# Layer 0 of a graph network on one core: the early part of the sums by source is put ahead of the second biases' rows

## The chip, the cores and the metric

The kernel runs on one core of one Trainium2 chip. The metric is the device time of one execution in microseconds, given as the median of several runs. Before the change it is 4813.85 us, the median of 3 runs (4810.83 to 4815.78).

## The reference

The program computes a network of four layers on 3125 nodes with 256 features and 100,000 edges. Each layer adds a graph convolution and an attention-like mix to the node features `x`, and then a feed-forward part. The change lies in the feed-forward part of layer 0, which is a mixture of 16 experts of which each node takes 2:

```python
gate_logits = x @ gate_w + gate_b
topk_vals, topk_idx = jax.lax.top_k(gate_logits, K)          # K = 2 of E = 16
topk_w = jax.nn.softmax(topk_vals, axis=-1)
h = jax.nn.relu(jnp.einsum('bsh,ehf->bsef', x, w1) + b1)
expert_out = jnp.einsum('bsef,efh->bseh', h, w2) + b2
sel = jnp.take_along_axis(expert_out, topk_idx[:, :, :, None], axis=2)
moe = jnp.sum(topk_w[..., None] * sel, axis=2)
y = x + moe
return (y - mu) / jnp.sqrt(var + EPS) * gamma + beta
```

Here `x` is the layer-normed input (`xn` in the kernel). One more piece is made in this stage although it belongs to layer 2: the graph convolution there needs the mean norm of all messages, `sum(|edge_weight| * norm(h[src])) / edges`. The kernel computes it as a sum over nodes, for which it needs, for every node, the sum of |edge_weight| over the edges that leave it. These are the "sums by source". They depend on the inputs alone, so they can be made at any time.

## The kernel before, in words

The nodes lie as 25 blocks of 125 (`NB`, `P`); `self.x` and `self.xn` are 125 x 25 x 256 in SBUF. The kernel is written with a tile framework: the program gives the operations, and a scheduler lays them into one queue for each engine at compile time. It takes the earlier operation in the program first where several are ready by its own clock, and may take a later one where the earlier ones still wait. Semaphores are added afterwards. On the chip each engine works off its queue in the order laid down.

`l0_ffn` (L1050) goes through these steps:

- The gates' best two (`top2`, L1062) and the place of each choice in a list sorted by expert (L1064 to L1114). The result is `slot` (L1114), 125 x 2 x 25 row numbers. The list is cut into 26 tiles of 384 rows (`NT`, `TS`), each tile belonging to one expert.
- The scatters (L1117): 50 indirect DMAs on GpSimd, one for each block and choice, write the rows of `xn` into `bx` in DRAM (`b0x_d` in the profile).
- `add_rows(beta)` (L1122, helper at L978): seven additions of `beta` to `x` on VectorE (L982).
- `times_rows` (L1124, helper at L285), called here "the second biases' rows": for seven pieces of four blocks it transposes the gates `g` (L291), copies them out of PSUM as `gt` (L293, recorded as L163 on VectorE or L165 on ScalarE), multiplies by the 16 x 256 matrix `b2` (L297), and adds the result to `xn` in place (L298). The addition to a block has to wait until both scatters of that block have read it.
- The early part of `weights_by_source` (L1128 to L1134, generator at L509). Its setup (L521 to L533) cuts weights and source numbers into bf16 keys. Then come groups of four columns of edges, 196 in all. Each group is five operations on VectorE (`lo` L537, `oh` L539, `ow` three times L543, each with three buffers) and four matmuls (L545) into one PSUM bank `ps`. The generator stops after each group; here it is run on until its share passes `EARLY` = 0.25. The block stands in `tc.issue_after(placed.ins)`, which puts its VectorE operations behind L1114 on VectorE and says nothing about other engines.
- The expert loop (L1142), 26 tiles. SP's queue is in program order here (`manual_schedule`, L1137): for each tile the loads of `w1`, `b1`, `w2` and of `xb` from `bx` (L1145 to L1151). TensorE transposes `xb` (L1156, 6 for each tile), VectorE copies to `xbt` (L1158), TensorE makes the hidden layer (L261), ScalarE its relu (L1163), TensorE the second product (L1168), and `evac` copies it out (L163 or L165) for a store to `by` (L1171). After each tile the loop advances the sums by source by their share (L1172).
- The gathers of `by` (L1180) with the weighting (L1183), and the closing norm.

PSUM is used in two pools of four banks: `self.bank()` (L150), from which `times_rows` and the sums take theirs, and the loop's own `pl` (L1136).

```python
placed = nc.vector.tensor_scalar(slot, sf, float(NT * TS - 1), None, op0=OP.min)
```

Of the kernel before, what the change touches and what calls it, by code (L numbers as in the profile page):

```python
# [109 lines left out]
class Net:  # L110
    NE, TS = 16, 384
# [938 lines left out]
    def l0_ffn(self, fast=False):  # L1050

        nc, tc, a = self.nc, self.tc, self.a
        NE, TS, ST, NT, bx = self.NE, self.TS, self.TS // 128, self.NT, self.bx
        by = self.dram.tile([NT * TS, D], F32, name="b0y_d")
        with ExitStack() as s:
            sb = s.enter_context(self.pool("f0_sb"))
            wk = s.enter_context(self.pool("f0_wk", 2))
            b2 = sb.tile([NE, D], F32, name="b2")
            nc.scalar.dma_start(b2, a["L0_ffn_b2"])
            gamma = self.load_b(sb, "L0_ffn_gamma")  # L1060
            beta = self.load_b(sb, "L0_ffn_beta")
            g, w, i8 = self.top2(sb, None, NE, P, NB, self.greatest)  # L1062
# [52 lines left out]
            for b in range(NB):  # L1115
                for j in range(2):
# [2 lines left out]
                        in_=self.xn[:, b, :], in_offset=None, bounds_check=NT * TS - 1, oob_is_err=False)  # L1119
                    tc.declare_no_dep(st.ins, group="slots", reason="each choice has a slot of its own")  # L1120
                    tc.add_to_no_dep_group("slots", st.ins)
            self.add_rows(beta)  # L1122
            y = self.xn
            self.times_rows(sb, g, b2, NE, y, self.xn)  # L1124
            with ExitStack() as s2:
                sums = None
                if fast:
                    sums = self.weights_by_source(s2.enter_context(self.pool("w_sb")),  # L1128
                                                  s2.enter_context(self.pool("w_wk", 3)), self.bank())

                    with tc.issue_after(placed.ins):
                        for part in sums:
                            if part > EARLY:
                                break  # L1134
                wk2 = s2.enter_context(self.pool("f0_t", 3))
                pl = s2.enter_context(self.pool("f0_ps", 4, space=PSUM))  # L1136
                s2.enter_context(tc.manual_schedule(engines={mybir.EngineType.SP}))  # L1137

                def bank():
                    return pl.tile([128, 512], F32, name="pl")  # L1140

                for i in range(NT):  # L1142
                    e = nc.sync.value_load(own[0:1, i:i + 1], min_val=0, max_val=NE - 1)
                    w1 = wk2.tile([128, HB, 512], F32, name="w1")
                    nc.sync.dma_start(w1, a["L0_ffn_w1"][ds(e, 1)].rearrange("o (c p) f -> p (o c) f", p=128))  # L1145
                    b1 = wk2.tile([128, 4], F32, name="b1")
                    nc.sync.dma_start(b1, a["L0_ffn_b1"][:, ds(e, 1), :].rearrange("p o f -> p (o f)"))
                    w2 = wk2.tile([128, 4, D], F32, name="w2")
                    nc.sync.dma_start(w2, a["L0_ffn_w2"][ds(e, 1)].rearrange("o (c p) f -> p (o c) f", p=128))
                    xb = wk2.tile([128, ST, D], F32, name="xb")  # L1150
                    nc.sync.dma_start(xb, bx[i * TS:(i + 1) * TS].rearrange("(t p) d -> p t d", p=128))  # L1151
                    xt = wk2.tile([128, HB, TS], F32, name="xbt", bufs=2)
                    for h in range(HB):
                        ps = bank()
                        for t in range(ST):
                            nc.tensor.transpose(ps[:, t * 128:(t + 1) * 128], xb[:, t, h * 128:(h + 1) * 128],  # L1156
                                                self.ident)
                        nc.vector.tensor_copy(xt[:, h, :], ps[:, :TS])  # L1158
                    hid = wk2.tile([128, 4, TS], F32, name="hid", bufs=2)
                    for f in range(4):  # L1160
                        ps = bank()
                        self.mm_feat(ps[:, :TS], w1[:, :, f * 128:(f + 1) * 128], xt, 0, TS)
                        nc.scalar.activation(hid[:, f, :], ps[:, :TS], AF.Relu, bias=b1[:, f:f + 1])  # L1163
                    yb = wk2.tile([128, ST, D], F32, name="yb", bufs=2)
                    for t in range(ST):
                        ps = bank()
                        for f in range(4):
                            nc.tensor.matmul(ps[:, :D], hid[:, f, t * 128:(t + 1) * 128], w2[:, f, :],  # L1168
                                             start=(f == 0), stop=(f == 3))
                        self.evac(yb[:, t, :], ps[:, :D])  # L1170
                    nc.scalar.dma_start(by[i * TS:(i + 1) * TS].rearrange("(t p) d -> p t d", p=128), yb)  # L1171
                    for part in sums or ():  # L1172
                        if i + 1 < NT and part > EARLY + (1 - EARLY) * (i + 1) / NT:
                            break
# [1250 lines left out]
```

## Time and profile before

| what | value |
|---|---|
| median of 3 runs | 4813.85 us |
| the profiled execution's own time | 4666.18 us |
| its span, first to last instruction | 4664.4 us |
| mean granted TensorE clock | 0.869 |
| busy share of PE / DVE / ACT / POOL | 80% / 54% / 28% / 22% |
| scatters (L1117) | 50, first at 808.71 us, last at 885.62 us |
| first transposes of the expert loop (L1156) | 892.9 us |
| first matmul of the expert loop (L261) | 926.8 us |
| last matmul of the expert loop (L1168) | 1274.0 us |

The profile shows one execution. Times are microseconds from the first instruction. PE is TensorE, PEld its weight loads, DVE VectorE, ACT ScalarE, POOL GpSimd and SP SyncE; a "q" after the name stands for the instructions of an engine's sequencer, such as the issue of a DMA. A row of the timeline gives start, busy time, engine, line, operation, output and inputs, how many were merged, and in brackets how long the engine was idle ahead of it and what released it. The profiled execution is 147.7 us shorter than the median of the runs that are only timed, so times of the profile are compared with times of the profile.

### The profile page before, as it was taken

The numbers are of one execution on the slowest core, as the hardware profiler recorded it, in microseconds if no ns is written. First come the engines' busy times: TensorE is split into PE (matmuls) and PEld (weight loads), VectorE is DVE, ScalarE is ACT, GpSimd is POOL, SyncE is SP. The second block draws the span as 40 slices with busy tenths as digits, with TensorE's granted clock in tenths as the row PEclk, the third lists the DMA queues.
The fourth block names the chain that finished last, engine by engine and source line by source line (L and its number), as shares of the span: only waits on it lengthen the run. The fifth ranks groups of instructions, "written<-read, shape, count | busy, mean of one in ns | idle before, by whom it ended". The sixth has DMA issues, their size and how long they took to land. (4 is left out here: it accounts for less than half of the span.)

```text
span 4664.4 us, 50401 instructions
## 1 busy us (share of the span) xinstructions
PE 3722.3 (80%) x16695; PEld 2505.9 (54%) x16695; DVE 2505.6 (54%) x8604; ACT 1302.8 (28%) x2336; POOL 1020.2 (22%) x1041
## 2 busy tenths in 40 slices
PE   1887796499938799999656566766799999999698
PEld 0676695277724556555545455655464444444466
DVE  5877317544475526994322323444265666777544
ACT  1367100022213223323100000000155655555521
POOL 2000000400055000000577777775000000000011
PEclk9786896599959799999877777887899999999699
DMA  6244630244332000000333333334102222221232
GB/s 176 75 113 118 138 82 22 81 135 140 107 85 40 4 29 9 13 14 7 106 105 106 104 104 104 104 104 139 58 7 59 59 63 56 63 52 49 74 107 68
DMA packets 256035, 358.86 MB, mean 77 GB/s; under 512 B 62719, under 2 KB 199350, under 8 KB 255765
## 3 DMA queue, kind: packets, MB, share of 16 engines
q1 hardware_dynamic: 135900, 176.07, 13.1%
q0 software_dynamic: 62832, 126.93, 10.3%
q10 hardware_dynamic: 57033, 52.54, 4.2%
q8 instruction: 136, 2.23, 0.2%
q14 instruction: 134, 1.10, 0.1%
HBM read 268.73 MB, written 94.97 MB: 78 GB/s over the span
## 5 line engine op out<-in xcount | busy, mean ns | idle before, releaser
L1601 POOL DMA_INDIRECT hg<-hx_d,idx x782 | 743.3, 950 | 282.8 <-issue 214.2
L1617 PE MATMUL acc<-hg,to 128*125 128x256 f32 x2042 | 584.5, 449 | 197.9 <-DVE to L1612 192.8
L1617 PEld LDWEIGHTS acc<-hg,to 128*125 128x125 f32 x2042 | 455.4, 227 | 309.3 <-DVE to L1612 216.3
L1971 PE MATMUL acc<-z,xr 125*65 125x500 f32 (+1 forms) x1400 | 577.4, 556 | 14.3 <-DVE z L1968 13.0
L1965 ACT ACTIVATE t<-xn,us 125x1000 f32<-125x1000 f32 (+1 forms) x400 | 409.4, 1037 | 239.0 <-DVE z L1968 228.1
L1968 DVE SCALAR_TENSOR_TENSOR z<-t,us,cs 125x1000 f32<-125x1000 f32 (+1 forms) x400 | 409.3, 1028 | 115.5 <-PE acc L1971 92.6
L1971 PEld LDWEIGHTS acc<-z,xr 125*65 125x65 f32 x1400 | 188.9, 145 | 314.8 <-issue 265.5
L1605 DVE TENSOR_TENSOR kw<-hg,awt 128x8 f32<-128x8 f32 x98 | 16.4, 168 | 581.2 <-DMA hg<-hx_d,idx 513.2
L261 PE MATMUL ps<-xt,w 128*128 128x500 f32 (+1 forms) x672 | 269.0, 547 | 1.8 <-DMA w<-in_L_ffn_W_dram 1.8
L1612 DVE TENSOR_SCALAR to<-iota_w,rel_b,kw 128x125 f32<-128x125 f32 (+1 forms) x782 | 245.2, 383 | 35.6 <-PE acc L1617 28.7
L1536 DVE SCALAR_TENSOR_TENSOR junk<-iota_w,rel_b,lock 128x125 f32<-128x125 f32 (+1 forms) x782 | 248.1, 386 | 0.0
L2255 POOL DMA_INDIRECT bx_d<-row,slot x25 | 31.2, 1248 | 891.3 <-ACT t L1965 422.9
L589 PE MATMUL ps<-y,cb 125*125 125x256 bf16 x1875 | 214.7, 279 | 0.0
L589 PEld LDWEIGHTS <-cb 125*125 125x125 bf16 x1875 | 213.5, 141 | 0.1
L797 ACT ACTIVATE k<-k 125x128 f32<-125x128 f32 x50 | 15.9, 318 | 687.0 <-DVE k L796 686.9
L190 ACT ACTIVATE rstd_t<-rstd_t 125x4 f32<-125x4 f32 (+2 forms) x86 | 17.2, 203 | 645.8 <-DVE rstd_t L189 630.2
L255 PE MATMUL ps<-wo,h 128*125 128x256 f32 x800 | 187.7, 386 | 3.6 <-ACT h L1439 2.6
L243 PE MATMUL ps<-ident,xn 125*128 125x125 f32 x300 | 58.8, 347 | 159.8 <-DVE xn L209 159.7
L1445 DVE SCALAR_TENSOR_TENSOR x<-ps,lg,x 125x256 f32<-125x256 f32 x200 | 92.7, 480 | 173.6 <-PE ps L255 173.6
L261 PEld LDWEIGHTS ps<-xt,w 128*128 128x128 f32 x672 | 122.7, 193 | 114.7 <-issue 102.4
L261 PE MATMUL ps<-h,w 128*128 128x500 f32 (+1 forms) x448 | 179.5, 541 | 2.3 <-ACT h L1434 1.6
L255 PEld LDWEIGHTS ps<-wo,h 128*125 128x125 f32 x800 | 142.9, 187 | 65.9 <-ACT h L1439 43.7
(566 smaller groups left out, 6326.7 us busy)
## 6 DMA issues: line engine op xcount, KB each, us to landing
cs<-ctt_d SPq DMA_DIRECT2D x150, 218.8 KB
w<-in_L_ffn_w_dram SPq DMA_DIRECT2D x52, 512.0 KB
cnt_d<-cd SPq DMA_DIRECT2D x25, 683.6 KB
cb<-cnt_d SPq DMA_DIRECT2D x25, 683.6 KB
ctt_d<-ct ACTq DMA_DIRECT2D x6, 2734.4 KB
hg<-hx_d,idx POOLq DMA_INDIRECT x782, 2.8
b0x_d<-zero SPq DMA_DIRECT2D x1, 9984.0 KB
xb<-b0x_d SPq DMA_DIRECT2D x26, 384.0 KB
```

Source lines behind the costliest of these rows:

```text
L243: self.nc.tensor.transpose(ps[:, j * P:(j + 1) * P], src[:, i // P + j, h * 128:(h + 1) * 128], self.ident[:P, :P])
L255: self.nc.tensor.matmul(ps, xt[:, h, b * P:(b + 1) * P], w[:, h, :], start=(h == 0), stop=(h == k - 1))
L261: self.nc.tensor.matmul(ps, w[:, h, :], xt[:, h, i:i + n], start=(h == 0), stop=(h == k - 1))
L589: nc.tensor.matmul(ps[:P, :D], cf[k][:, h * P:(h + 1) * P], y3[:, b0 + k, j, :], start=(k == 0 and j == 0), stop=(k == m - 1 and j == 2))
L1445: nc.vector.scalar_tensor_tensor(self.x[:, b, :], ps[:P, :D], g[:, b, e:e + 1], self.x[:, b, :], op0=OP.mult, op1=OP.add)
L1536: nc.vector.scalar_tensor_tensor(junk[:, :m * P], self.iota_w[:, :m * P], rel[:, c:c + 1], lock[:, b:b + m].rearrange("p b n -> p (b n)"), ...
L1601: nc.gpsimd.indirect_dma_start(out=hg[:, j, :], out_offset=None, in_=hx, in_offset=bass.IndirectOffsetOnAxis(ap=idx[:, c0 + j:c0 + j + 1], ...
L1612: nc.vector.tensor_scalar(to, self.iota_w[:, :nb * P], rel[:, c:c + 1], kw[:, j:j + 1], op0=OP.is_equal, op1=OP.mult)
L1617: nc.tensor.matmul(acc[k], to[:, (k - b) * P:(k - b + 1) * P], hg[:, j, :D], start=(c == first[k]), stop=(c == last[k]))
L1965: nc.scalar.activation(t[:, :n], rows[:, k4, :n], AF.Relu, bias=us[:, 2, b, k4:k4 + 1], scale=us[:, 0, b, k4:k4 + 1])
L1968: nc.vector.scalar_tensor_tensor(z[:, :n], t[:, :n], us[:, 1, b, k4:k4 + 1], c, op0=OP.add, op1=OP.mult)
L1971: nc.tensor.matmul(acc[h, k][:, :w], xr[:, b, k4, :], z[:, k * PW:k * PW + w], start=(b == 0), stop=(b == NB - 1))
```

## The change

The calls of `add_rows` and `times_rows` move from the place ahead of the early part of the sums to the place behind it, still ahead of the expert loop and its pools. Nothing is added or taken away.

```diff
-            self.add_rows(beta)
             y = self.xn
-            self.times_rows(sb, g, b2, NE, y, self.xn)
             with ExitStack() as s2:
                 sums = None
                 if fast:
...
                         for part in sums:
                             if part > EARLY:
                                 break
+                self.add_rows(beta)
+                self.times_rows(sb, g, b2, NE, y, self.xn)
                 wk2 = s2.enter_context(self.pool("f0_t", 3))
                 pl = s2.enter_context(self.pool("f0_ps", 4, space=PSUM))
                 s2.enter_context(tc.manual_schedule(engines={mybir.EngineType.SP}))
```

In program order the operations are then: the scatters, the sums' setup and 49 of their groups, the seven additions of `beta`, the biases' rows, the expert loop. Two things follow from the order of calls itself: the sums' PSUM bank is taken from `self.bank()` ahead of those of `times_rows`, and the two pools of the sums (`w_sb`, `w_wk`) are open while `times_rows` runs.

## The prediction

> **What bounds the kernel now.** I read the page first for the share of each engine, then the busy time by stretches around the edit, then the queues of VectorE (DVE), TensorE (PE) and SyncE (SP) in order of time. On the page PE is busy 80% of a span of 4664.4 us, but the edit touches one stage only, so that stage decides. By stretches (busy us, granted clock, DMA share, GB/s):
>
> ```profile
> core 0: us, PE busy (x) PEld busy (x) DVE busy (x) ACT busy (x) POOL busy (x), PEclk, DMA share, GB/s
> 808.00:890.00 82.00, 30.92 (x83) 14.66 (x84) 26.33 (x71) 1.70 (x3) 63.18 (x50) 0.50 0.33 92
> 890.00:925.00 35.00, 19.39 (x170) 14.36 (x170) 34.01 (x207) 0.00 (x0) 0.00 (x0) 0.50 0.30 95
> 1000.00:1100.00 100.00, 98.09 (x507) 74.49 (x506) 43.83 (x221) 21.54 (x41) 0.00 (x0) 1.00 0.43 135
> ```
>
> Three stages with three owners. From 808 to 890 the 50 scatters own the time (one every 1.5 us on POOL) and DVE is idle for 56 us. From 890 to 925 DVE owns it (34.0 of 35 us): it makes the early sums. After that the expert loop is PE-bound (98%) at about 13.3 us a tile.
>
> The idle DVE of the first stage is the wait of the biases' add (L298) for the scatters that still read xn, in the list of waits:
>
> ```profile
> DVE xn L298 <- DMA b0x_d<-xn,slot: 54.0, 25, 5.3
> ```
>
> The DVE queue: the last biases' add, then groups of five operations every 0.82 us (897.87 to 898.69), and only at 926.19 the first copy that the expert loop needs:
>
> ```profile
> 889.47 0.42 DVE L298 TENSOR_TENSOR xn<-ps,xn 125x256 f32<-125x256 f32 x1 [1.83 <-DMA b0x_d<-xn,slot]
> ...
> 897.87 0.44 DVE L543 TENSOR_TENSOR ow<-oh,part 128x100 bf16<-128x100 bf16 x3
> 898.23 0.20 DVE L539 TENSOR_TENSOR oh<-i,key 128x100 bf16<-128x100 bf16 x1
> 898.35 0.41 DVE L537 TENSOR_TENSOR lo<-i,key 128x512 bf16<-128x512 bf16 x1
> ...
> 926.19 0.56 DVE L1158 COPY xbt<-pl 128x384 f32<-128x384 f32 x1
> ```
>
> The PE queue shows the order in which the scheduler laid the work down:
>
> ```profile
> 878.86 1.21 PE L297 MATMUL ps<-b,gt 16*125 16x256 f32 x2 [0.37 <-DVE gt L163]
> 880.93 1.01 PE L545 MATMUL ps<-ow,lo 128*128 128x75 bf16 x12 [0.86 <-DVE xn L298]
> ...
> 891.46 0.44 PE L545 MATMUL ps<-ow,lo 128*128 128x75 bf16 x4 [0.70 <-DVE ow L543]
> 892.92 0.47 PE L1156 MATMUL pl<-ident,xb 128*128 128x128 f32 x1 [1.02 <-DMA xb<-b0x_d]
> 893.19 0.47 PE L545 MATMUL ps<-ow,lo 128*128 128x75 bf16 x4
> ...
> 926.80 1.65 PE L261 MATMUL pl<-xbt,w 128*128 128x384 f32 x2
> ```
>
> The reader is to see that tile 0's six transposes (L1156), which come in the program after all 49 early groups, stand in PE's queue behind only seven of them (12 + 4 x 4 matmuls up to 891.46). The scheduler puts an instruction where its own clock says that the inputs are there, not where the program has it. On SP the load of xb for tile 0 waits for the last scatter:
>
> ```profile
> 889.40 0.38 SPq L1151 DMA_DIRECT2D xb<-b0x_d  x1
> 890.58 0.37 SPq L1145 DMA_DIRECT2D w<-in_L_ffn_w_dram  x1
> ```
>
> So the prize is at most the stretch from the transposes (about 895) to the first expert matmul (926.80).
>
> **What the Trainium skill says.** "TensorE: Matmul & The Clock Gate", Step-by-step: matmuls stay in program order, only weight loads are pulled ahead. The trace agrees: the matmul of group 8 starts at 893.19, after the transpose that waited for its DMA. Same page, What's actually happening: a cold PE runs at half clock, and gets the full one after about 3.4 us of sustained work. Here L261 takes 1006 ns at 926.8 and 486 later, and the granted clock goes from 0.50 to 1.00. "DMA: Bandwidth & Descriptors", Anatomy of one DMA: a semaphore wait of a DMA is held on the issuing sequencer; SP's 889.40 with tile 1's weights behind it agrees. "SBUF — State Buffer", Who interferes with whom: tensor_tensor with two SBUF inputs meets GpSimd only where that reads SBUF, while casts and tensor_scalar can lock it out. Here scatters take 1.19 us, 1.36 to 1.56 beside some casts and two-input operations (L524, L526, L532, L533), 1.31 and 1.32 beside two groups of sums.
>
> **The change, part by part.** No operation is added or removed.
>
> *The sums' setup* (L521 to L533, 12 DVE operations: 1.04 + 0.91 + 0.56 + 0.96 + 0.72 + 1.03 + 0.56 + 0.71 + 0.56 + 1.36 + 0.56 + 0.96 = 9.9 us, 9.2 from start to start) no longer alternates with the biases' adds; it runs from 808.8 to about 818, under the scatters. Cost: none. Its loads of src and weights were issued on SP at 774.65 and 775.06, ahead of everything here; they stay.
>
> *The early groups*: 49 (the first with (c+4)/782 over 0.25 is c = 192), 49 x 0.82 = 40 us of DVE. Before, five were made by 890 and 44 after, 44 x 0.82 = 36 us on the path. If PE let them, all would be done by 818 + 40 = 858.
>
> *Where PE lets them.* Tile 0's transposes will again be put where the scheduler's clock sees xb loaded. That clock can be read from the old order: between the slots and that place it packed on DVE the setup (9.2 us), 25 adds (0.34 start to start, 8.5), three copies of gt (1.4) and about seven groups (5.7), so 25 us, and up to 28 with idle time that the order does not show. The scatters and the load don't depend on what moves, so the place is the same on that clock: in the new order 9.2 of setup and (25..28 - 9.2) / 0.82 = 19 to 23 groups stand ahead of the transposes. I take 22 (estimate). On the chip the scatters take 80 us, not that. PE reaches the transposes near 838 and waits there until xb lands at 892.9, and queued behind it are 27 groups of sums and nearly all of the biases' matmuls. DVE can go three groups further (three buffers), then waits too: 49 - 25 = 24 groups are left, from about 894 on: 24 x 0.82 = 19.7, to 913.7.
>
> *The biases' rows* (L291, L297, L298): their bank is now one of three, since the sums' bank is taken first, so about three blocks are multiplied ahead, and their adds stand on DVE behind the sums. 22 blocks and 21 transposes are left on PE, at a time when PE is what bounds. At full clock: two passes of 5.34/24 = 0.22 us each, 22 x 0.445 = 9.8, and 21 x 0.84/6 = 2.9, together 12.7. At half clock, from their own rows (2.04 us for two blocks, 1.0 for four transposes): 22.4 + 6 = 28.4. Below nothing isn't possible, since the work was wholly hidden before. I take 16: mostly full clock, with a few us cold or waiting for an add. The 22 adds (0.34 each, 7.5 us) fit under it.
>
> *add_rows* (seven of up to 1.22 us) moves too, but was run at 782 to 791, while DVE waited for the gates, and can still be; nothing. If that cover went, 8 us of DVE.
>
> *POOL and SP*: the same instructions in the same order. Denser DVE work from 808 to 838 may add 0.1 us to some 20 scatters: 0 to 3 us, taken 0.5. Tile 1's and 2's weights landed by 902 and stay early enough.
>
> *Sum*: the expert stream can start, counted as PE time, at 913.7 + 0.5 + 16 = 930.2 against 926.8: 3.4 us later, with 0.5 for the scatters about **4 us slower**. The profiled execution would go from 4666.18 (span 4664.4 and 1.8 around it) to 4670. The median of the runs, 4813.85, is 147.7 us longer; I put the same difference on it: **4817.9**.
>
> **The rivals.**
> *Clean win*: the transposes stay behind the biases on PE. For it: that is the program's order, and the sums would be done by 858, the adds, held by the scatters, by 890. Then tile 0's copy comes near 895.5 instead of 926.2: -31 us, 4783. Against it: the seven groups in the old order.
> *Half win*: all sums, but not the biases, stand ahead of the transposes: 892.9 + 1.9 + 16 = 910.8, -16 us, 4798.
> *Slower*: the biases' matmuls run cold and in single steps between adds, interleaved with tile 0's: 913.7 + 0.5 + 28.4 = 942.6, +16 us, 4830. It decides once they cost PE over 22 us (926.8 + 9.6 - 914.2). For it: the clock is 0.50 up to 929 in the old trace. Against: tile 0 gives PE dense work in between.
>
> **How the numbers follow.** Forecast 0.60, clean win 0.17, half win 0.07, slower 0.16. About 0.2% (9.6 us) is what a measurement of this kernel can tell from no change. The forecast's own range is 4810 to 4828 (12.7 or 24 us for the biases, three groups either way); of its 0.60, 0.52 lie within 0.2%, 0.07 above, 0.01 below. Faster: 0.17 + 0.07 + 0.01 = 0.25; same 0.52; slower 0.07 + 0.16 = 0.23. Leaving out the win (0.17) and half of the slower case (0.08) would be too much, so the range runs from 4780 to 4830.
>
> **What would show it.** Right: L1156 waits some 50 us for xb, in PE's queue after 19 to 26 groups of L545; L298 mostly after 913; L297 between matmuls of L261. Wrong: L545 runs through to 860 and L1158 stands near 895.

## The result, and the profile after

The kernel after took 4840.48 us, the median of 5 runs (4836.20 to 4867.77), beside 4813.85 us before (5 runs, 4808.00 to 4827.43): a ratio of 1.0065, 95% interval 1.0036 to 1.0095. It is slower by some 27 us, where 4 were forecast. The profiled execution is the slowest of the five (4867.77, span 4865.9); the four others lie between 4836 and 4842.

Two things have to be set aside when profiles are compared. In some executions the gathers of layer 2 (L1601), far behind the change, last some 150 us longer: 988 us from first to last in the profile of before, 1137 us in that of after. The timed runs of before are 147.7 us longer than its profile, which fits the longer form. So whole spans of these two profiles say nothing here. And the profile of after reaches the stage 6 us later (slots, L1114, at 814.2 against 808.2), which lies ahead of the change. I therefore measure from the slots to the first gather behind the expert loop (L1180), and split that at the first transposes of tile 0 (L1156).

The stretches of after, the first, second and last of them the ones shown of before, two put in between (columns: the stretch, its length, busy time of PE, weight loads, DVE, ACT, POOL, then granted clock, DMA share, GB/s):

```profile
core 0: us, PE busy (x) PEld busy (x) DVE busy (x) ACT busy (x) POOL busy (x), PEclk, DMA share, GB/s
808.00:890.00 82.00, 11.47 (x100) 8.18 (x100) 37.03 (x162) 0.00 (x0) 65.21 (x34) 0.50 0.23 64
890.00:925.00 35.00, 3.58 (x29) 2.95 (x30) 3.43 (x21) 0.00 (x0) 19.18 (x17) 0.50 0.43 125
925.00:941.00 16.00, 9.03 (x78) 6.38 (x76) 16.00 (x95) 0.00 (x0) 0.00 (x0) 0.50 0.22 74
941.00:975.00 34.00, 34.00 (x82) 19.48 (x81) 13.15 (x42) 3.87 (x7) 0.00 (x0) 0.50 0.05 15
1000.00:1100.00 100.00, 97.70 (x523) 74.21 (x523) 46.71 (x235) 20.71 (x40) 0.00 (x0) 1.00 0.43 136
```

By 890 POOL had done all 50 scatters before; now it has done 34 of them, with as much busy time, and from 890 to 925 PE and DVE do almost nothing. The list of waits of the stage names what they stood for:

```profile
PEld pl L1156 <- DMA xb<-b0x_d: 75.8, 1, 75.8
DVE lo L537 <- PE ps L545: 75.8, 1, 75.8
```

In PE's queue stand 24 groups (the first at 825.25) and then the transposes, close to the forecast's 19 to 23, but these wait until 920.16:

```profile
844.09 0.45 PE L545 MATMUL ps<-ow,lo 128*128 128x75 bf16 x4 [0.37 <-DVE ow L543]
920.16 1.11 PE L1156 MATMUL pl<-ident,xb 128*128 128x128 f32 x4 [75.62 <-DMA xb<-b0x_d]
921.06 0.47 PE L545 MATMUL ps<-ow,lo 128*128 128x75 bf16 x4
...
945.48 2.77 PE L261 MATMUL pl<-xbt,w 128*128 128x384 f32 x4
948.18 3.77 PE L297 MATMUL ps<-b,gt 16*125 16x256 f32 x8
951.88 1.00 PE L291 MATMUL ps<-ident,g 125*16 125x125 f32 x4
952.68 2.77 PE L261 MATMUL pl<-xbt,w 128*128 128x384 f32 x4
```

DVE stops three groups later, because its next `lo` waits for PE to have read an earlier one, and goes on behind the transposes:

```profile
845.59 0.20 DVE L539 TENSOR_TENSOR oh<-i,key 128x100 bf16<-128x100 bf16 x1
921.57 0.43 DVE L537 TENSOR_TENSOR lo<-i,key 128x512 bf16<-128x512 bf16 x1 [75.77 <-PE ps L545]
```

POOL's queue holds the surprise. A scatter takes 1.19 us; the fifth takes 21.92:

```profile
822.70 1.94 POOL L1117 DMA_INDIRECT b0x_d<-xn,slot  x1 [0.31 <-issue]
824.94 21.92 POOL L1117 DMA_INDIRECT b0x_d<-xn,slot  x1 [0.30 <-issue]
847.17 1.18 POOL L1117 DMA_INDIRECT b0x_d<-xn,slot  x1 [0.30 <-issue]
```

It ends at 846.86, 1.07 us after DVE's last operation (845.59 + 0.20). That is the time of one undisturbed scatter: it looks as though it did nothing until DVE stopped. SP issues the load of xb at 916.64, 102.4 us after the slots, where it was 81.2 before (889.40 - 808.2).

### The profile page after: what moved, and what is told of

Same layout as the page of the kernel before. It is cut to its first block, busy times and chain, and to the rows that moved or that the text cites. A ratio compares the mean times of both kernels' runs of the same rounds, so it can differ in the third digit from the quotient of the medians.

```text
span 4865.9 us, 50397 instructions
## 1 busy us (share of the span) xinstructions
PE 3759.0 (77%) x16695; PEld 2514.4 (52%) x16695; DVE 2512.6 (52%) x8604; ACT 1302.1 (27%) x2336; POOL 1041.1 (21%) x1041
## 5 line engine op out<-in xcount | busy, mean ns | idle before, releaser
L1601 POOL DMA_INDIRECT hg<-hx_d,idx x782 | 743.1, 950 | 431.5 <-issue 212.8
L1617 PE MATMUL acc<-hg,to 128*125 128x256 f32 x2042 | 598.3, 448 | 293.9 <-issue 147.6
L1617 PEld LDWEIGHTS acc<-hg,to 128*125 128x125 f32 x2042 | 443.9, 224 | 427.5 <-issue 176.9
L470 PE MATMUL t<-ky,lo 128*128 128x75 bf16 (+4 forms) x1251 | 138.8, 253 | 38.7 <-ACT ct L473 24.1
```

What stands on the lines that cost most here:

```text
L470: nc.tensor.matmul(t[:, w * 25 * r:(w + 1) * 25 * r], lo[:, :, n % 4], ky[:, :25 * r, n % 4], start=(j == 0), stop=(j == ws[w0 + w][2] - 1))
L1601: nc.gpsimd.indirect_dma_start(out=hg[:, j, :], out_offset=None, in_=hx, in_offset=bass.IndirectOffsetOnAxis(ap=idx[:, c0 + j:c0 + j + 1], ...
L1617: nc.tensor.matmul(acc[k], to[:, (k - b) * P:(k - b + 1) * P], hg[:, j, :D], start=(c == first[k]), stop=(c == last[k]))
```

## The experiments

The stage in each profile, one execution each, in us. "Before again" and "after again" are b_again and a_again below.

| kernel | slots to transposes | transposes to first gather | slots to first gather | against before |
|---|---|---|---|---|
| before | 84.7 | 385.5 | 470.2 | |
| before again | 85.6 | 386.7 | 472.3 | +2.1 |
| after | 105.9 | 408.4 | 514.3 | +44.1 |
| after again | 106.0 | 389.4 | 495.5 | +25.3 |
| e1_order | 124.1 | 348.7 | 472.8 | +2.7 |
| e2_late | 106.0 | 388.1 | 494.1 | +23.9 |
| e3_early0 | 85.4 | 400.1 | 485.5 | +15.3 |
| e6_f32 | 124.0 | 348.6 | 472.6 | +2.4 |
| e5_psum | 107.1 | 348.6 | 455.6 | -14.6 |
| e4_weave2 | 86.0 | 353.6 | 439.6 | -30.6 |

**My theory after the first look**: DVE's sums hold POOL's scatter for as long as they run without a gap (+21 us), and the biases' rows, hidden before, now lie on PE at half clock (+23). Below, "cold" is a granted clock of 0.50 and "warm" one near 1.00. **Rivals**: the transposes' place in PE's queue is the loss, so that the clean win is there once they stand behind; the biases' matmuls alternating cold with tile 0's are the loss; the long scatter is chance.

**b_again: the kernel before, once more**, for the spread of the stage.

> The kernel before, profiled a second time. If the 147.7 us between the first profile (4666.18) and the runs without one lie in a stage of layer 2 that varies from run to run (its gathers lasted 987 us in the profile of before and 1136 in that of after), this profile may show the longer one, near 4814; if the profile of before is typical, it comes near 4666 again. Either way the scatters last 78 us from first to last landing, each 1.2 us, and the first matmul of the expert loop comes 40 us after the last scatter.

4663.28 us beside 4664.94, one execution each. The stage differs by 2.1 us, so I take differences of the table of 3 us and less as nothing.

**a_again: the kernel after, once more.**

> The changed kernel, on the same chip as a run of the one before. In its first profile the last matmul of the expert loop came 50 us later than before, 6 to 7 of them from a stage ahead of the change. Theory 'held-off scatters and cold biases': about 21 us from one scatter held off for 22 us, about 23 us from the biases' rows on a PE that runs at half clock, so +43 us (+0.9%), and the same two in this profile. If only the measured ratio of the first comparison counts, +31 us (1.0065).

4834.65 us (4825.09 to 4847.97) beside 4811.8 (30 runs): ratio 1.004, interval 1.0027 to 1.0054. There is again one scatter of 21.92 us, so it isn't chance:

```profile
819.51 21.92 POOL L1117 DMA_INDIRECT b0x_d<-xn,slot  x1 [0.31 <-issue]
```

But the part behind the transposes now loses only 4.0 us, where the first profile of after lost 22.9. PE's queue shows the difference: the same order of work, at full clock from about 943 on.

```profile
940.15 2.77 PE L261 MATMUL pl<-xbt,w 128*128 128x384 f32 x4
942.85 2.15 PE L297 MATMUL ps<-b,gt 16*125 16x256 f32 x8
944.93 0.59 PE L291 MATMUL ps<-ident,g 125*16 125x125 f32 x4
945.36 1.46 PE L261 MATMUL pl<-xbt,w 128*128 128x384 f32 x4
946.75 1.99 PE L297 MATMUL ps<-b,gt 16*125 16x256 f32 x8
```

Eight passes of L297 take 1.99 us here and 3.77 above; in the first profile the clock stayed at 0.50 from 941 to 975 with PE busy for 34.00 of 34 us. In all, PE spends 18.6 us on the biases' rows behind the transposes here and 29.6 in the first profile. So the change costs about 25 us in the usual execution and 44 in the cold one, which fits the timed medians of +23 and +27 and the one run at 4867.77.

**e1_order: the kernel after, tile 0's transposes forced behind the last of the biases' products on PE.** This is the clean win's order.

```
+                self.last_mm = nc.tensor.matmul(ps[:P, :D], gt[:, j * P:(j + 1) * P], rows, ...)
...
+                        with tc.issue_after(self.last_mm.ins):
                             for t in range(ST):
                                 nc.tensor.transpose(...)
```

> The changed kernel with the transposes of xb put behind the last matmul of the biases in PE's queue; nothing else is changed. Theory 'PE's order is all that is wrong' (the clean win of the prediction): the sums run through to about 860, the adds follow the scatters, -31 us against the kernel before. Theory 'the sums hold the scatters off': nothing stops VectorE now, so one scatter lasts some 40 us, the other 45 follow at 1.5 us, the last lands near 930, and the time is 5 to 10 us over that of before; the biases' rows are hidden again.

4813.56 us (4804.18 to 4828.79): ratio 1.0001, interval 0.9993 to 1.001. Behind the transposes it is 36.8 us shorter. Of these, 32.2 are the clean win: the first expert matmul now follows the transposes after 1.6 us instead of 33.9, since all early sums and biases are done ahead. The rest comes from nine groups of sums that the scheduler also drew ahead of the loop. But DVE, no longer stopped by PE, runs 49 groups on end, and the scatter is held for all of them:

```profile
820.14 1.94 POOL L1117 DMA_INDIRECT b0x_d<-xn,slot  x1 [0.30 <-issue]
822.38 39.94 POOL L1117 DMA_INDIRECT b0x_d<-xn,slot  x1 [0.30 <-issue]
```

```profile
861.05 0.21 DVE L539 TENSOR_TENSOR oh<-i,key 128x100 bf16<-128x100 bf16 x1
861.17 0.66 DVE L163 COPY gt<-ps 16x500 f32<-16x500 f32 x1
```

The transposes come 39.4 us later. The scatter ends at 862.32, 1.06 us after the end of the last operation of the sums (861.05 + 0.21), although DVE goes on at once with a copy of gt out of PSUM. So gain and loss are both there and cancel: the queue's order alone does not bring the clean win, and the price of the sums under the scatters is their own length.

**e2_late: the kernel after, with one piece of the biases' rows behind each of tiles 1 to 7** instead of all within tile 0.

```
-                self.times_rows(sb, g, b2, NE, y, self.xn)
...
+                    if 0 < i <= len(PIECES):
+                        self.times_rows(sb, g, b2, NE, y, self.xn, PIECES[i - 1:i])
```

> The changed kernel with the biases' rows not ahead of the expert loop but one piece after each of tiles 1 to 7, where PE runs at full clock. Theory 'cold clock': their 22.9 us become the 12.7 us that the prediction worked out for full clock, so about 10 us under the changed kernel, still 30 us over the one before. Rival 'they cost PE as much anywhere': no gain over the changed kernel.

4831.59 us (4826.02 to 4852.56): ratio 1.0039, interval 1.0023 to 1.0055. It is no different from after, and the 10 us that I expected aren't there. Behind the transposes it is 1.4 us shorter than a_again: beside a warm execution of after, it makes no difference that can be told where in the loop the biases' matmuls are.

**e3_early0: the kernel before with no early sums** (EARLY = 0.0). All sums go to the expert loop.

> The kernel before with EARLY at 0: one group of the sums ahead of the expert loop, the other 48 early ones spread over its tiles. The 36 us of VectorE between the last scatter and the first expert matmul go, and PE pays about 0.43 us for each of 44 more groups in the loop, 19 us: -17 us (-0.35%) against before. If the loop's VectorE can't take them, less.

4829.94 us (4822.36 to 4836.74): ratio 1.0039, interval 1.0025 to 1.0053, a miss. The transposes come 85.4 us after the slots, as before, and the expert matmuls start at 899.1, right behind the transposes at 897.5, but the loop gives back more than that. Two stretches of this kernel, then the second of them in before (the first stands in the prediction):

```profile
1000.00:1100.00 100.00, 93.13 (x494) 68.85 (x493) 52.51 (x279) 19.12 (x37) 0.00 (x0) 0.97 0.40 124
1100.00:1200.00 100.00, 93.89 (x483) 69.92 (x482) 46.99 (x247) 18.18 (x35) 0.00 (x0) 0.93 0.37 116
```

```profile
1100.00:1200.00 100.00, 97.82 (x520) 73.60 (x519) 49.33 (x252) 21.17 (x41) 0.00 (x0) 1.00 0.46 142
```

With more groups in each tile PE is busy 93% instead of 98%, and the clock is 0.93 to 0.97. From the first expert matmul to the first gather it takes 398.5 us against 351.6: 47 us for 40 more groups (the trace has eight ahead of that matmul, where before has 48), so about 1.2 us a group where I had counted 0.43 of PE time. These groups are dearer in the loop than the 0.82 us they cost on DVE ahead of it. That isn't a fixed price: in e1_order nine groups fewer than before save 4.5 us there, 0.5 us each.

**lk_tt, lk_t4, lk_ps, lk_ts: the cost of DVE's work for a scatter, by itself.** Into the kernel before, right behind the slots, go idle DVE operations, back to back, whose results nobody reads. The code is that of lk_tt; lk_t4 has 33 comparisons of an fp32 tile with itself, lk_ps 40 copies of fp32 out of PSUM, lk_ts 100 tensor_scalar on bf16. Each is one execution. The adds are held behind the idle work, so whole times (4706.63, 4694.89 and 4695.48 us beside 4664.94; 4842.27 beside 4812.01) tell little here.

```
...
+                with tc.issue_after(placed.ins):
+                    for k in range(58):
+                        self.idle = nc.vector.tensor_tensor(jo[k % 2], ja, jk[:, None, :].to_broadcast([128, 128, 4]), op=OP.is_equal)
...
```

> The kernel before with 58 idle VectorE operations of the form of lo (bf16, two SBUF inputs, 0.34 us each, 20 us in all) put without a gap right behind the slots, and the biases' adds behind them. They feed nothing. Theory 'VectorE holds off the scatters': one scatter lasts until the 58 are through, 15 to 20 us, and the whole row of 50 ends some 15 to 20 us later than before. Rival 'the long scatter of the changed kernel has another cause': all scatters stay at 1.2 us, and the adds, which wait for scatters anyway, end as before.

> The same with 33 operations in float32 with two SBUF inputs (128x512, about 0.6 us each, 20 us in all). If it is the second SBUF input that holds the scatters off, it is as with bf16: 15 to 20 us. If it is a fast mode that only 16-bit operands have, the scatters stay at 1.2 to 1.5 us.

> The same with 40 copies from PSUM to SBUF in float32 (128x400, 0.5 us each, 20 us in all), that is no SBUF input at all. Theory 'VectorE holds off the scatters through SBUF inputs': the scatters stay at 1.2 us and end as before. Rival 'any VectorE work without a gap holds them off': 15 to 20 us later.

> The kernel before with 100 idle bf16 operations with one SBUF operand (tensor_scalar, 512 elements) on VectorE right behind the slots, back to back, the biases' additions behind them; compare with lk_tt (two operands, one scatter of 18.45 us) and lk_ps (none longer). Theory that the second SBUF operand matters: all scatters at 1.19 to 1.5 us. Rival that the bf16 rate alone matters: a scatter as long as the idle work.

The idle work and POOL's queue, for lk_tt (bf16, two operands in SBUF):

```profile
814.99 19.53 DVE L1131 TENSOR_TENSOR jo<-ja,jk 128x512 bf16<-128x512 bf16 x58
```

```profile
815.39 1.46 POOL L1134 DMA_INDIRECT b0x_d<-xn,slot  x1 [32.96 <-DVE slot L1126]
817.15 18.45 POOL L1134 DMA_INDIRECT b0x_d<-xn,slot  x1 [0.30 <-issue]
835.90 1.19 POOL L1134 DMA_INDIRECT b0x_d<-xn,slot  x1 [0.30 <-issue]
```

For lk_t4 (fp32, two operands in SBUF):

```profile
814.19 19.95 DVE L1131 TENSOR_TENSOR jg<-jf 128x512 f32<-128x512 f32 x33
```

```profile
816.29 1.47 POOL L1134 DMA_INDIRECT b0x_d<-xn,slot  x1 [0.30 <-issue]
818.07 1.49 POOL L1134 DMA_INDIRECT b0x_d<-xn,slot  x1 [0.31 <-issue]
```

For lk_ts (bf16, one operand):

```profile
814.92 26.24 DVE L1131 TENSOR_SCALAR jo<-ja 128x512 bf16<-128x512 bf16 x100
```

```profile
816.87 1.29 POOL L1134 DMA_INDIRECT b0x_d<-xn,slot  x1 [0.30 <-issue]
818.46 1.27 POOL L1134 DMA_INDIRECT b0x_d<-xn,slot  x1 [0.30 <-issue]
```

In lk_ps (fp32 copies out of PSUM for 19.33 us) the scatters beside them take 1.19 to 1.24 us. So neither a busy DVE nor its bf16 rate holds a scatter. Of the four kinds only the bf16 operation with two operands in SBUF does, and then until 1.08 us (835.60 - 834.52) after the last of them; the last scatter of lk_tt begins 92.9 us after the slots, in the three others 75.3 to 78.5. That is just the kind of every operation of the sums.

Two limits. The first scatter of lk_tt begins 0.40 us into the idle work and still takes only 1.46 us, with 17.7 us of that work to come; the next one is held. In after and e1_order too, a scatter that begins just ahead of the sums ends beside them (822.70 + 1.94, with the sums from 823.97 on). So not every scatter beside this kind of work is held, and why the next one is, the runs don't show. And lk_t4 differs from lk_tt in more than the type: it reads one tile twice, where lk_tt reads two, the second one repeated along the row. That the type decides, and not this, is not shown by the four alone.

**e5_psum: e1_order with the early groups' counting table in a PSUM bank, in fp32, and the small one-hot in fp32.**

```
...
+        i4w = wide.rearrange("p (a b) -> p a b", b=4)
+        nc.vector.tensor_copy(i4w, i4)
...
+            it = i4w if early else i4
-            nc.vector.tensor_tensor(lo, i4, key[...], op=OP.is_equal)
+            nc.vector.tensor_tensor(lo, it, key[...], op=OP.is_equal)
...
```

> e1_order with the early groups' comparisons (L537, L539) reading their counting table from a PSUM bank in fp32 instead of from SBUF in bf16, and the small one-hot in fp32; the three products of a group (100 elements wide) still read SBUF twice. A group on VectorE should last about 1.0 to 1.3 us instead of 0.82: 50 groups, 50 to 65 us, inside the 85 us from slots to xb. Theory (what holds the scatter is bf16 work with two operands in SBUF): no scatter over 2 us, slots to the first transposes 85 to 90 us instead of e1_order's 124, the loop as in e1_order (349 us): slots to first gather 435 to 445 against before's 470, ratio 0.993 to 0.995. Rival (any VectorE work without a gap holds it): one scatter of 50 us and more, slots to transposes 135 us, slower than e1_order by 10 us.

4798.12 us (4786.71 to 4809.49): ratio 0.9968, interval 0.9955 to 0.998. The long hold is gone: beyond the first few beside the setup, no scatter takes over 2.4 us, and the last begins 893.14 - 809.76 = 83.4 us after the slots, where it is 117.0 in e1_order (928.64 - 811.67) and 77.4 before (885.62 - 808.21). The loop is that of e1_order (348.6). But the transposes come at 107.1 us, not 85 to 90, and not for the scatters: a group now takes 1.29 us instead of 0.82, the sums end at some 883, and the adds are queued behind them on DVE, so that PE multiplies the biases only then, at half clock, until 916:

```profile
911.20 3.77 PE L297 MATMUL ps<-b,gt 16*125 16x256 f32 x8 [0.22 <-ACT gt L165]
914.90 0.38 PE L291 MATMUL ps<-ident,g 125*16 125x125 f32 x1
915.08 0.27 PE L551 MATMUL ps<-ow,lo 128*128 128x75 bf16 x1
915.67 1.21 PE L297 MATMUL ps<-b,gt 16*125 16x256 f32 x2 [0.33 <-DVE gt L163]
916.82 1.54 PE L1163 MATMUL pl<-ident,xb 128*128 128x128 f32 x6
```

With the same order of work, taking away the bf16 pair of SBUF operands moved the stage from +2.7 to -14.6 us. That supports the cause within the kernel itself. There the second operand is still one that is repeated along the row, so that alone does not hold a scatter. What holds up the transposes next is the biases.

**e6_f32: the same table as an fp32 tile in SBUF.** As built, its switch was off when the groups were made, so its operations are those of e1_order (its trace has the bf16 `lo<-i,key` throughout).

> As e5_psum, but the table is an fp32 tile in SBUF (and the one-hot stays bf16): both operands in SBUF, one of them fp32. A group about 1.0 us. Theory that the bf16 pair of operands is what holds the scatter: scatters at most some 1.5 us as in lk_t4, slots to transposes 85 to 95 us, ratio 0.993 to 0.997. Rival that two SBUF operands of any type hold it, or that the short bf16 products are enough: one scatter of about 50 us, ratio 1.001 or slower.

4812.78 us (4804.15 to 4829.10): ratio 1.0004, interval 0.9994 to 1.0014, with one scatter of 39.95 us. It is a second e1_order and nothing more; what an fp32 table in SBUF does in the sums themselves was not tried.

**e4_weave2: two groups of sums behind each add of the biases but the last** (`each` takes two steps of the sums' generator, one more group goes ahead), each add behind the groups ahead of it, and the transposes behind the last product, as in e1_order.

```
...
+                    if each:
+                        behind.enter_context(self.tc.issue_after(self.last_ow.ins))
                     last = nc.vector.tensor_add(out[:, b, :], ps[:P, :D], add[:, b, :])
+                if each and b < NB - 1:
+                    with self.tc.issue_after(last.ins):
+                        each()
...
```

> The kernel before, with the sums' 50 early groups no longer behind the biases' rows but between them: two groups on VectorE after each of L298's additions, tile 0's transposes behind the last of the biases' products. Each addition waits for its own block's scatters, so VectorE has a gap at every block. Theory (VectorE's bf16 two-input work holds an indirect scatter only until the next gap): a scatter is held for at most the 1.64 us of two groups, 25 blocks, so the scatters are longer by 0 to 41 us in all (likeliest 15, as each block's two scatters take some 2.4 us with gaps of their own), the loop keeps the 37 us that e1_order gained: between -31 and +10 us against before, about -15. Rival (any VectorE work beside the scatters costs its own length): +41 on the scatters, ratio 1.001. Rival (the loop's gain is not there): slower.

4781.22 us (4780.96 to 4787.11): ratio 0.9938, interval 0.9915 to 0.996, faster than both kernels. An add waits for the scatters of its own block, so DVE has a gap for each block, and the scatters run on beside the sums (DVE's queue, then POOL's):

```profile
842.21 0.42 DVE L301 TENSOR_TENSOR xn<-ps,xn 125x256 f32<-125x256 f32 x1 [0.76 <-DMA b0x_d<-xn,slot]
842.55 0.41 DVE L543 TENSOR_TENSOR lo<-i,key 128x512 bf16<-128x512 bf16 x1
842.89 0.20 DVE L545 TENSOR_TENSOR oh<-i,key 128x100 bf16<-128x100 bf16 x1
...
844.76 0.42 DVE L301 TENSOR_TENSOR xn<-ps,xn 125x256 f32<-125x256 f32 x1 [0.34 <-DMA b0x_d<-xn,slot]
```

```profile
840.95 1.19 POOL L1123 DMA_INDIRECT b0x_d<-xn,slot  x1 [0.31 <-issue]
842.44 1.19 POOL L1123 DMA_INDIRECT b0x_d<-xn,slot  x1 [0.30 <-issue]
843.94 1.19 POOL L1123 DMA_INDIRECT b0x_d<-xn,slot  x1 [0.30 <-issue]
```

First to last scatter takes 78.4 us (813.9 to 892.3) against 76.9 before (808.7 to 885.6), and the part behind the transposes keeps 31.9 of the 36.8 us. That is the clean win's 31 us, by the same operations in another order: the first expert matmul again follows the transposes after 1.6 us, and the loop has about as many groups of sums as before. The 15 us that I had set aside for the scatters were not needed: once the setup is over, none takes over 1.43 us.

## Why the prediction was wrong

- *Place of the transposes* (19 to 23 groups ahead, 22 taken): right in kind, one group beyond the range. The trace has 24. Their wait for xb was 75.6 us, not some 50, for the scatters.
- *What is left behind them* (24 groups, 19.7 us): right. They run on DVE from 921.57 to 940.5, 19 us.
- *The biases' rows on PE* (16, with 12.7 warm and 28.4 cold): right in the usual execution, by the sum more than by its parts. All 25 blocks were left behind the transposes, not 22, and PE spent 18.6 us on them in a_again. From the transposes on, a_again is 4.0 us behind before, where the sum ahead of its scatter term gave 3.4 (with a 0.5 that the prediction doesn't name). The cold figure has a slip: 21 transposes at 1.0 us for four are 5.3 us, not 6. In the profile of after the loss is 22.9, the case that the "slower" rival described: cold, alternating with tile 0's. I had argued that tile 0's dense work warms PE; it did in one profile and not in the other, with the same order.
- *The setup* and *add_rows*: nothing, as stated, as far as the split of the stage shows.
- **The step that failed** is "POOL and SP": "Denser DVE work from 808 to 838 may add 0.1 us to some 20 scatters: 0 to 3 us, taken 0.5." It is 21.3 (106.0 in a_again against 84.7), and 39.4 where the sums run through. I had bounded it from two scatters beside groups of sums (1.31 and 1.32 us) and from the Trainium skill, "SBUF — State Buffer", Who interferes with whom. Both misled. In the kernel before, the sums beside a scatter are bursts of at most 0.8 us between adds, with DVE idle for about two us behind each. I scaled the delay by a short burst as if it were a rate; nearly 27 groups without a gap (21.8 us) are one scatter of 21.92 us. The page says that tensor_tensor with both inputs in SBUF contends with a GpSimd instruction that reads SBUF, for the whole instruction, and infers that descriptor generation is spared. The trace lists `slot`, in SBUF, as an input of each scatter, so the first part may apply; but a block for one instruction would be 0.34 us here, and 58 of them in bf16 held a scatter for 18.45. It also has tensor_scalar as a kind that can lock GpSimd out; 100 of them left the scatters at 1.3 us. Here the measurement decides.
- *The clean win* lost for a reason I hadn't named. I argued against it by the place of the transposes alone; with that mended (e1_order) it still comes to 1.0001, for the scatters. *Slower* got the sign right and came nearer in size, with +16 us where +27 and +23 were measured, but in the usual execution that is luck: its mechanism, the cold biases, wasn't there, and the held scatter made the loss.

A scatter of before beside such a burst; the one of after beside the long run stands above (824.94, 21.92 us):

```profile
862.91 1.32 POOL L1117 DMA_INDIRECT b0x_d<-xn,slot  x1 [0.30 <-issue]
```

Summed for the usual execution: 3.4 + 21.3 = 24.7, and a_again has 25.3.

**What stays open**: why the clock stayed at 0.50 for some 40 us in one execution and rose at 942.8 in another; what in the chip a scatter waits for; why the first scatter beside such work still passes; and whether it is the bf16 type alone that makes the difference between lk_tt and lk_t4. The same section of the Trainium skill says that a DMA which a DVE operation stalls is one whose descriptors GpSimd makes, and that the two engines share a pair of ports which one holds to the end of its instruction. The first fits the trace (the scatters are issued on POOL). For the second, the runs show only which kind of operation holds a scatter and when it lets go; that the hold spans many instructions without a gap is not what "for the whole instruction" says.

## What to carry to other kernels

An idle engine beside another's DMA isn't free room: before moving work there, ask whether it is of a kind that holds that DMA, and how long it runs without a gap, since a trace that has only short bursts shows the price of a burst and not of a run. If the work must go there, lay it between operations that wait for the DMA anyway; the gaps then come by themselves. With the transposes forced behind the biases as well, this gave 0.9938 where the plain move gave 1.0065. And a scheduler's clock that thinks a load early parks the instructions that wait for it ahead of work that is ready, so look at the built queues and not at the program's order.

## What the runs showed of the hardware

- An indirect scatter, issued by POOL, of 1.19 us: 18.45, 21.92 and 39.94 us beside bf16 tensor_tensor without a gap and with both operands in SBUF, ending 1.06 to 1.08 us after the last of them; 1.5 beside fp32 tensor_tensor of one tile with itself; 1.3 beside bf16 tensor_scalar; 1.19 to 1.24 beside copies out of PSUM.
- In lk_tt the scatter that began 0.40 us into that work took 1.46 us; the next one was held. In e4_weave2, with 1.8 us of it at a time, none was held (at most 1.43 us once the setup was over).
- In e5_psum the three products of a group read two SBUF operands, one fp32 and one bf16, between comparisons that read PSUM; no scatter beside them took over 2.4 us.
- The clock stayed at 0.50 in one profile for 34 us in which PE was busy without a gap (941 to 975).
- In the expert loop 40 more groups of sums went with a clock of 0.93 to 0.97 instead of 1.00 and cost about 1.2 us each (e3_early0); nine fewer saved 0.5 us each (e1_order).
